# Cross-attention on a decoder layer: scores on four 32-row strips of the array, values in one run, and one written order for four engines

## The chip, the cores and the metric

The kernel runs on one core of a Trainium2 chip. The metric is device time in microseconds of one execution; three runs of the kernel before gave 1502.5, 1503.64 and 1507.64 us, a median of 1503.64. Engines are named as the profile names them: PE (TensorE; PEld are its weight loads), DVE (VectorE), ACT (ScalarE), POOL (GpSimd), SP (the sync engine, here only a DMA queue).

## The reference, cut to what matters

One decoder layer with the norm after each part, batch 2, 2048 tokens, width 512, 16 heads of 32:

```python
x = layernorm(x + ssd(x))                  # state-space mixer: Y[0] / norm @ W_out.T
x = layernorm(x + xattn(x, ctx))           # 16 heads, ctx has 77 rows, causal mask, softmax
x = layernorm(x + slots(x))                # 16 slots read x, 16 experts (512-2048-512), x reads the slots

# xattn
q = (x @ q_w + q_b);  k = (ctx @ k_w + k_b);  v = (ctx @ v_w + v_b)     # split in 16 heads of 32
att = softmax(mask(q @ k.T / sqrt(32)));  y = att @ v;  return y @ o_w + o_b
```

The change lies in the second line and the part of the third in which the slots read x (dispatch and collect below).

## The kernel before, in words

There are four stages, one behind the other. The first computes the state-space mixer and, between its steps, small set-ups (`setup()`): keys `kbh`/`kbl` and values `vt` of both batches among them. The second, here called the attention stage, is the one that the change rewrites. The third streams 192 weight slabs of 1 MB of the 16 experts through 23 slab places in SBUF. The fourth lets the tokens read the slots and writes the output.

Most matrices are held as a pair of fp32r tiles, the rounded value (`h`) and the rest (`l`). A product of two pairs is three matmuls (`three`): over a contraction of 512 that is 12 matmuls.

The attention stage goes over 16 token tiles n of 256 rows (`TB`), each as two strips s of 128 rows. One tile consists of these pieces; the letters are those that the changed source uses:

- load: DMAs of x, of the mixer's output `Ud` and of its factor `fd` (12 in all, on SP's queue)
- S, `scaled`: POOL multiplies, ACT rounds, POOL takes the rest
- O, `out_proj`: 12 matmuls of 512 columns, then DVE adds and the norm's steps on DVE and ACT
- X, `x1_transposed`: four PE transposes, ACT and DVE split them; POOL adds the output bias
- Q, `queries`: 24 matmuls of 256 columns for two groups of four heads, ACT and DVE split
- W, `weigh`: scores and softmax of four heads per call. Four heads share a matmul: `kbh` holds the keys of four heads in a block diagonal of 128 rows by 4 x 77 columns, and three matmuls of 308 columns (h by h, h by l, l by h) give the scores of four heads. Then a maximum on DVE, exponentials on ACT (for odd groups a subtraction and a sum on DVE), a reciprocal on DVE, a product on POOL
- G, `gather`: four PE transposes of the weights, copied to `pt` by ACT (three of four groups) or DVE (group 2)
- V, `values`: four matmuls per group into 32 columns of the array each; with the fourth group the result is split
- P, `o_proj`: 12 matmuls of 512 columns, norm, x2 written to HBM by a DMA that ACT issues, split
- Y, `x2_transposed`; D, `dispatch` (24 matmuls of 256 columns, running maximum and sum); T, `p_transposed`; C, `collect` (12 matmuls of 512 columns into the sums `Z`)

PSUM's eight banks are one for `y` (values), two for `mm` (O, Q, P, D, C), two for `tr` (transposes) and two for `sc` (scores).

The order in which the pieces are emitted is a table of eight beats per tile (`plan`), with written-out lists for the first and last pieces (`head`, `drain`). The whole program then goes through a scheduler with a timeline of its own, which decides the order of the instructions on each engine; that is why pieces lie interleaved on PE, for instance scores between the matmuls of a query block.

Expert slabs are placed in the order of `first`; a slab's DMA waits until the tiles of the attention stage that lie in the same SBUF bytes are done with, and SP's queue runs in order.

Of the kernel before, what the change touches and what calls it, by code (L numbers as in the profile page):

```python
# [16 lines left out]
S = 77  # L17
NE, FF = 16, 2048
# [3 lines left out]
TB = 256  # L22
# [12 lines left out]
DEFPLAN = [  # L35
    ["W", "V", ["scaled", 0, 0], ["x2_transposed", 3, 1], ["queries", 1, 0], "G"],
    ["W", "V", ["scaled", 0, 1], ["dispatch", 3], "G"],
    ["W", "V", ["o_proj", 2, 0], "G"],
    ["W", "V", ["p_transposed", 3], ["queries", 1, 1], "G"],
    ["L", "W", "V", ["x2_transposed", 2, 0], ["out_proj", 0, 0], "G"],  # L40
    ["W", "V", ["out_proj", 0, 1], "G"],
    ["W", "V", ["x1_transposed", 0, 0], ["o_proj", 2, 1], "G"],
    ["W", "V", ["x1_transposed", 0, 1], ["collect", 3], "G"]]
# [33 lines left out]
def weave(flows, depth, lag):  # L77
# [3 lines left out]
    while flows or live:  # L81
# [4 lines left out]
        for f in list(live):  # L86
# [6 lines left out]
TUNED = {'plan': [['W', ['x2_transposed', 3, 1], 'V', 'G'], ['V', 'W', 'G', ['scaled', 0, 0]],  # L93
          ['G', ['out_proj', 0, 0], ['queries', 1, 0], 'W', 'V', ['dispatch', 3]], ['W', ['o_proj', 2, 0], ['queries', 1, 1], 'G', 'V'],
          ['G', 'V', 'W', ['scaled', 0, 1], ['x2_transposed', 2, 0]], ['V', ['p_transposed', 3], 'W', 'G'],
          ['W', 'V', ['out_proj', 0, 1], ['x1_transposed', 0, 0], 'G'],
          ['V', ['x1_transposed', 0, 1], ['o_proj', 2, 1], 'L', 'G', 'W', ['collect', 3]]],
 'E': {'uf': 2,
# [15 lines left out]
 'lg': 1,  # L114
 'lv': 2,
 'dv': [1, 3],
 'first': 'ABCD067451892GH3JIFEKLM',
# [63 lines left out]
 'head': [['load', 0], ['scaled', 0, 0], ['out_proj', 0, 0], ['load', 1], ['scaled', 0, 1], ['scaled', 1, 0], ['x1_transposed', 0, 0],  # L181
          ['out_proj', 0, 1], ['out_proj', 1, 0], ['x1_transposed', 0, 1], ['queries', 0, 0], ['queries', 0, 1], ['weigh', 0, 0, 0], ['load', 2],
          ['weigh', 0, 0, 2], ['gather', 0, 0, 0], ['scaled', 1, 1], ['weigh', 0, 0, 1], ['values', 0, 0, 0], ['out_proj', 1, 1], ['gather', 0, 0, 2],
          ['x1_transposed', 1, 0], ['gather', 0, 0, 1], ['values', 0, 0, 1], ['weigh', 0, 0, 3], ['x1_transposed', 1, 1], ['weigh', 0, 1, 0],
          ['values', 0, 0, 2], ['gather', 0, 1, 0], ['weigh', 0, 1, 1], ['weigh', 0, 1, 2], ['scaled', 2, 0], ['out_proj', 2, 0], ['gather', 0, 0, 3],
          ['queries', 1, 0], ['weigh', 0, 1, 3], ['values', 0, 0, 3], ['gather', 0, 1, 1], ['o_proj', 0, 0], ['gather', 0, 1, 2], ['values', 0, 1, 0],
          ['queries', 1, 1], ['scaled', 2, 1], ['weigh', 1, 0, 0], ['gather', 0, 1, 3], ['x1_transposed', 2, 0], ['weigh', 1, 0, 1],
          ['values', 0, 1, 1], ['values', 0, 1, 2], ['values', 0, 1, 3], ['x2_transposed', 0, 0], ['gather', 1, 0, 0], ['weigh', 1, 0, 2],
          ['values', 1, 0, 0], ['out_proj', 2, 1], ['gather', 1, 0, 1], ['load', 3], ['values', 1, 0, 1], ['weigh', 1, 0, 3], ['o_proj', 0, 1],
          ['x1_transposed', 2, 1], ['gather', 1, 0, 2], ['x2_transposed', 0, 1], ['weigh', 1, 1, 0], ['values', 1, 0, 2], ['gather', 1, 0, 3],  # L190
          ['scaled', 3, 0], ['values', 1, 0, 3], ['weigh', 1, 1, 1], ['gather', 1, 1, 0], ['out_proj', 3, 0], ['weigh', 1, 1, 2], ['queries', 2, 0],
          ['gather', 1, 1, 1], ['values', 1, 1, 0], ['dispatch', 0], ['o_proj', 1, 0], ['queries', 2, 1], ['weigh', 1, 1, 3], ['gather', 1, 1, 2]],
 'drain': [['values', 12, 1, 1], ['gather', 12, 1, 3], ['values', 12, 1, 2], ['weigh', 13, 0, 0], ['scaled', 14, 1], ['x2_transposed', 12, 0],
           ['values', 12, 1, 3], ['weigh', 13, 0, 1], ['p_transposed', 11], ['gather', 13, 0, 0], ['x1_transposed', 14, 0], ['weigh', 13, 0, 2],
           ['values', 13, 0, 0], ['out_proj', 14, 1], ['gather', 13, 0, 1], ['values', 13, 0, 1], ['x1_transposed', 14, 1], ['load', 15],
           ['o_proj', 12, 1], ['gather', 13, 0, 2], ['weigh', 13, 1, 0], ['weigh', 13, 0, 3], ['weigh', 13, 1, 1], ['values', 13, 0, 2],
           ['collect', 11], ['x2_transposed', 12, 1], ['gather', 13, 0, 3], ['gather', 13, 1, 0], ['values', 13, 0, 3], ['scaled', 15, 0],
           ['out_proj', 15, 0], ['gather', 13, 1, 1], ['weigh', 13, 1, 2], ['values', 13, 1, 0], ['dispatch', 12], ['queries', 14, 0],
           ['weigh', 13, 1, 3], ['gather', 13, 1, 2], ['scaled', 15, 1], ['o_proj', 13, 0], ['queries', 14, 1], ['values', 13, 1, 1],
           ['gather', 13, 1, 3], ['values', 13, 1, 2], ['weigh', 14, 0, 0], ['x2_transposed', 13, 0], ['p_transposed', 12], ['values', 13, 1, 3],  # L200
           ['weigh', 14, 0, 1], ['gather', 14, 0, 0], ['weigh', 14, 0, 2], ['values', 14, 0, 0], ['out_proj', 15, 1], ['x1_transposed', 15, 0],
           ['gather', 14, 0, 1], ['values', 14, 0, 1], ['x1_transposed', 15, 1], ['o_proj', 13, 1], ['gather', 14, 0, 2], ['weigh', 14, 0, 3],
           ['collect', 12], ['x2_transposed', 13, 1], ['weigh', 14, 1, 0], ['gather', 14, 0, 3], ['values', 14, 0, 2], ['values', 14, 0, 3],
           ['weigh', 14, 1, 1], ['queries', 15, 0], ['gather', 14, 1, 0], ['gather', 14, 1, 1], ['weigh', 14, 1, 2], ['dispatch', 13],
           ['values', 14, 1, 0], ['weigh', 14, 1, 3], ['o_proj', 14, 0], ['queries', 15, 1], ['gather', 14, 1, 2], ['values', 14, 1, 1],
           ['gather', 14, 1, 3], ['values', 14, 1, 2], ['x2_transposed', 14, 0], ['values', 14, 1, 3], ['weigh', 15, 0, 0], ['p_transposed', 13],
           ['weigh', 15, 0, 1], ['o_proj', 14, 1], ['gather', 15, 0, 0], ['weigh', 15, 0, 2], ['values', 15, 0, 0], ['gather', 15, 0, 1],
           ['weigh', 15, 0, 3], ['gather', 15, 0, 2], ['x2_transposed', 14, 1], ['values', 15, 0, 1], ['collect', 13], ['weigh', 15, 1, 0],
           ['weigh', 15, 1, 1], ['values', 15, 0, 2], ['weigh', 15, 1, 2], ['gather', 15, 0, 3], ['values', 15, 0, 3], ['gather', 15, 1, 0],
           ['gather', 15, 1, 1], ['dispatch', 14], ['values', 15, 1, 0], ['weigh', 15, 1, 3], ['o_proj', 15, 0], ['gather', 15, 1, 2],  # L210
           ['values', 15, 1, 1], ['gather', 15, 1, 3], ['x2_transposed', 15, 0], ['values', 15, 1, 2], ['values', 15, 1, 3], ['p_transposed', 14],
           ['o_proj', 15, 1], ['collect', 14], ['x2_transposed', 15, 1], ['dispatch', 15], ['p_transposed', 15], ['collect', 15]],
 'pme': 0,
 'b1': 27,
# [3 lines left out]
 'x2': 2,  # L218
 'zt': 2,
 'qb': 2}  # L220
# [3 lines left out]
def tile_decoder(ctx, tc, a, out, dbg=None, upto=9, opt=None):  # L224
# [56 lines left out]
    kbh, kbl = ([kv_[b].tile([128, 4, 4 * S], FR, name=f"kb{t}{b}") for b in range(B)] for t in "hl")  # L281
# [11 lines left out]
    with ExitStack() as st:  # L293
# [121 lines left out]
        def setup():  # L415
# [20 lines left out]
            for b in range(B):  # L436
                for h in range(2):
                    m2 = slice(2 * h, 2 * h + 2)
                    kf = sb.tile([128, 2, 4, S], FP, tag="sw", bufs=2, name="kf")
                    pool.memset(kf, 0.0)  # L440
                    for r in range(4):
                        sr = slice(32 * r, 32 * r + 32)
                        dve.tensor_copy(kf[sr, :, r, :], kst[sr, m2, b * S:b * S + S])
                    split(kbh[b][:, m2].rearrange("p m (r s) -> p m r s", s=S), kbl[b][:, m2].rearrange("p m (r s) -> p m r s", s=S), kf, pool)
                    yield
# [254 lines left out]

    with ExitStack() as st:
        psb = {tag: st.enter_context(tc.tile_pool(name="b_" + tag, bufs=n, space=PSUM, reuse_waits="tile"))
               for tag, n in (("y", 1), ("mm", 2), ("tr", 2), ("sc", 2))}
        sbq, sb1, sb0 = (st.enter_context(tc.tile_pool(name=nm, bufs=1, side="right", reuse_waits="tile"))
                         for nm in ("b_q", "b_x1T", "b_in"))
        sbz, sbx, sb = (st.enter_context(tc.tile_pool(name=nm, bufs=1, side="right", reuse_waits="tile"))
# [125 lines left out]
        def values(n, s, hg):  # L832
            b = n // NT
            if hg == 0:
                ts[n]["y", s] = PT("y", bufs=1)
# [95 lines left out]
        def period(p):  # L931

            for q8, items in enumerate(PLAN):
                for it in items:
# [8 lines left out]
                    if 0 <= op_[1] < N:  # L943
                        yield op_
# [650 lines left out]
```

## Time and profile before

| what | value |
|---|---|
| median of 3 runs | 1503.64 us |
| the profiled execution's own time | 1507.68 us |
| its span, first to last instruction | 1505.3 us |
| mean granted PE clock | 0.949 |
| first stage, 0 to 305 us: PE, DVE busy; DMA share | 277.36, 262.41; 0.90 |
| attention stage, middle, 480 to 780 us: PE, DVE, ACT busy | 298.27, 244.62, 179.89 |
| expert stage, 928 to 1410 us: PE busy; DMA share, GB/s | 396.08; 1.00, 409 |
| last stage, 1410 to 1505 us: PE, DVE busy | 78.19, 75.88 |

How to read it: the profile is one execution, with its time beside the runs' median. Busy times of PE count pipelined matmuls, so a busy PE may still have room; the start-to-start times of its timeline tell what one instruction costs in a stream. "Waits" are idle stretches of an engine with the instruction whose end let it go on. The "chain of waits" is the work that ended last, followed back from the end. A row such as `ACT pt L234 <- PE tr L828: 20.1, 24, 2.3` reads: ACT's copy to `pt` waited 20.1 us in 24 waits for PE's transposes, 2.3 us at the longest.

### The profile page before, as it was taken

The page shows a single profiled execution, that of the slowest core. Times are in us where ns is not written, and L with a number is a line of the kernel's source. Part 1 is how long each engine was busy: PE and PEld are TensorE (multiplying, and loading weights), DVE is VectorE, ACT ScalarE, POOL GpSimd, SP SyncE. Part 2 cuts the span into 40 slices and gives each one's busy share as a digit, 9 for nine tenths or more (in the row PEclk, how much of TensorE's full clock was granted, in tenths as well). Part 3 has the DMA queues.
Part 4 walks back from the last instruction along what each step waited for, and adds up shares of the span by engine and source line. Part 5 has one row for each costly group of instructions (what it writes and reads, how often), then busy time and mean ns, then how long its engine had stood idle before and what let it go on. Part 6 is the DMA issues. An engine that isn't in the chain of part 4 may idle for free.

```text
span 1505.3 us, 27732 instructions
## 1 busy us (share of the span) xinstructions
PE 1351.7 (90%) x10442; PEld 994.8 (66%) x10442; DVE 912.4 (61%) x2150; ACT 620.1 (41%) x1685; POOL 447.5 (30%) x496
## 2 busy tenths in 40 slices
PE   7899999979999999999999997948987977889896
PEld 6788889867878888888888875205653544532365
DVE  7997997857788888888887764002111111134497
ACT  5534544525655566565656552001010000034256
POOL 4634543634444444444443311000000000000045
PEclk9999999988999999999999998969998998999899
DMA  9889978993212121322210249998999999999547
GB/s 319 210 196 239 231 198 213 242 273 92 72 57 63 58 63 57 92 57 65 64 43 15 71 153 358 363 416 363 399 418 420 418 418 419 418 421 420 226 145 261
DMA packets 188061, 339.64 MB, mean 226 GB/s; under 512 B 12347, under 2 KB 135739, under 8 KB 163096
## 3 DMA queue, kind: packets, MB, share of 16 engines
q1 hardware_dynamic: 171632, 311.25, 59.7%
q10 hardware_dynamic: 16296, 26.62, 5.2%
q8 instruction: 83, 1.36, 0.4%
q14 instruction: 50, 0.41, 0.1%
HBM read 299.56 MB, written 38.27 MB: 224 GB/s over the span
## 4 chain that ended last, share of the span: by engine, by line
PE 58%; DVE 17%; DMA 15%; ACT 5%; issue 3%; POOL 1%; SPq 1%; ACTq 0%; POOLq 0%; DVEq 0%
PE mm L231 26%; DMA ew<-in_e_W 10%; PE up L231 6%; PE pj L231 4%; PE tr L828 3%; DVE X L530 3%; PE yac L231 3%; PE sc L231 3%; PE y L231 2%; DMA ew<-in_e_Wg 2%; PE fo L231 1%; PE uu L231 1%; DVE C L530 1%; PE gp L231 1%; ACT pp L818 1%
## 5 line engine op out<-in xcount | busy, mean ns | idle before, releaser
L231 PE MATMUL up<-ew,hT 128*32 128x512 f32 x944 | 131.3, 639 | 35.5 <-DMA ew<-in_e_W 32.1
L820 POOL TENSOR_TENSOR pp<-pp,den 128x308 f32<-128x308 f32 x128 | 89.4, 703 | 158.6 <-DVE den L819 106.2
L1185 POOL MEMSET aT<- 128x512 f32 x16 | 8.3, 524 | 404.7 <-PE yac L231 403.0
L1176 ACT ACTIVATE sv<-up 128x512 f32<-128x512 f32 x32 | 19.1, 597 | 247.2 <-PE up L231 234.2
L231 PE MATMUL mm<-xTh,cqh 128*128 128x256 f32 x256 | 76.3, 308 | 26.1 <-ACT xTh L234 26.1
L231 PEld LDWEIGHTS up<-ew,hT 128*32 128x32 f32 x944 | 27.2, 113 | 101.8 <-issue 66.0
L1235 DVE TENSOR_TENSOR Qc<-mm,vec 128x512 f32<-128x512 f32 x32 | 22.1, 691 | 113.3 <-PE mm L231 113.3
L242 DVE TENSOR_TENSOR xTl<-tr,xTh 128x512 fp32r<-128x512 f32 x32 | 21.3, 689 | 109.2 <-ACT xTh L234 109.1
L828 PE MATMUL tr<-cst,pp 128*77 128x128 f32 x512 | 81.9, 285 | 1.9 <-DVE x1Tl L724 1.2
L234 ACT COPY pt<-tr 77x512 f32<-77x512 f32 x96 | 55.7, 583 | 63.2 <-PE tr L828 35.4
L231 PE MATMUL mm<-x1Th,w30h 128*128 128x256 f32 x256 | 76.7, 301 | 5.0 <-ACT x1Th L723 2.6
L818 ACT ACTIVATE pp<-sc,mx 128x77 f32<-128x77 f32 x240 | 75.5, 327 | 12.2 <-DVE mx L815 11.4
L231 PEld LDWEIGHTS mm<-xTh,cqh 128*128 128x128 f32 x256 | 51.3, 205 | 40.4 <-ACT xTh L234 29.5
L231 PE MATMUL mm<-xTl,cqh 128*128 128x256 f32 x256 | 76.6, 301 | 1.2 <-DVE xTl L242 1.2
L231 PE MATMUL mm<-x1Tl,w30h 128*128 128x256 f32 x256 | 74.4, 291 | 0.5 <-DVE x1Tl L724 0.5
L231 PE MATMUL mm<-xTh,cql 128*128 128x256 f32 x256 | 74.8, 294 | 0.0
L231 PE MATMUL mm<-x1Th,w30l 128*128 128x256 f32 x256 | 73.8, 288 | 0.0
L828 PEld LDWEIGHTS tr<-cst,pp 128*77 128x77 f32 x512 | 60.5, 150 | 16.8 <-issue 11.1
L530 DVE SCALAR_TENSOR_TENSOR X<-raw,vec,X 128x256 f32<-128x256 f32 x80 | 66.4, 876 | 5.5 <-ACT X L526 5.0
L231 PE MATMUL yac<-ew,aT 128*32 128x512 f32 x488 | 65.1, 652 | 4.7 <-issue 4.2
L746 POOL TENSOR_TENSOR ut<-ut,fb 128x512 f32<-128x512 f32 x32 | 41.2, 1291 | 73.7 <-DMA ut<-Ud 43.2
L242 POOL TENSOR_TENSOR yyl<-ut,yyh 128x512 fp32r<-128x512 f32 x32 | 41.1, 1285 | 68.3 <-ACT yyh L234 67.5
(376 smaller groups left out, 4329.2 us busy)
## 6 DMA issues: line engine op xcount, KB each, us to landing
ew<-in_e_W SPq DMA_DIRECT2D x119, 1024.0 KB, 15.0
ew<-in_e_Wg SPq DMA_DIRECT2D x60, 1024.0 KB, 12.9
BS<-scrBc SPq DMA_DIRECT2D x48, 256.0 KB, 4.9
CS<-scrC SPq DMA_DIRECT2D x48, 256.0 KB, 6.3
xs<-in_xT SPq DMA_DIRECT2D x32, 256.0 KB, 5.7
xt<-in_x SPq DMA_DIRECT2D x32, 256.0 KB, 2.7
ut<-Ud SPq DMA_DIRECT2D x32, 256.0 KB, 3.3
fb<-fd SPq DMA_DIRECT2D x128, 64.0 KB, 3.1
```

Source lines behind the costliest of these rows:

```text
L231: return pe.matmul(o, lhsT=l, rhs=r, start=start, stop=stop, **kw)
L234: (act.copy, dve.tensor_copy, pool.tensor_copy)[e](o, i)
L242: (lo_eng or dve).tensor_tensor(lo, src, hi, ALU.subtract)
L530: dve.scalar_tensor_tensor(dst, raw[:, j, 1 + t:1 + t + TB], w4[:, t:t + 1], dst, ALU.mult, ALU.add)
L746: (act, dve, pool)[EN.get('uf', 1)].tensor_tensor(ut, ut, fb, ALU.mult)
L818: act.activation(pp[:, r, :], sv[:, r, :], AF.Exp, bias=mx[:, h:h + 1], accum_out=den[:, h:h + 1])
L820: (act, dve, pool)[EN.get('d%d' % hg, 2)].tensor_tensor(pp, pp, den[:, h4].unsqueeze(2).to_broadcast([128, 4, S]), ALU.mult)
L828: pe.transpose(tp[0:S, r * 128:r * 128 + 128], pp[:, r, :], ident)
L1176: last["silu"] = act.activation(sv, up, AF.Silu)
L1185: pool.memset(aT, 0.0)
L1235: dve.tensor_tensor(Qc[b][:, mp * 2:mp * 2 + 2, t1:t1 + TB], qq, vec[:, V_CQ + mp * 2:V_CQ + mp * 2 + 2].unsqueeze(2).to_broadcast([128, 2 ...
```

## The change

- *Scores on four strips of rows.* The keys are no longer a block diagonal. `kbh`/`kbl` hold each group of heads in 80 columns (`SP`), head r in partitions 32r to 32r + 31. `weigh(n, s)` now does all 16 heads of a strip in one call with 48 matmuls of 80 columns, each over 32 contraction rows; head r of every group lands in bank r of a score tile of four banks, of which there is one.
- *Values in one run.* `values(n, s)` does the 16 matmuls of a strip together, into an `mm` bank; the `y` bank is gone, so PSUM is two `mm`, two `tr`, four `sc`.
- *Order.* Every piece is now its PE part, and generators for its steps on the other engines. `serve` walks a string of letters (`ORDER`), PE's order, with times of each step (`WORK`) and buffer counts (`ROOM`), and returns all steps sorted by the time at which its model starts them. The steps are emitted in that order, and from the thirteenth PE piece on each instruction of PE, ACT, DVE and POOL is tied to the one before it on its engine, so that the scheduler keeps the order. `plan`, `head` and `drain` are gone.
- *Moved and resized.* All `pt` copies are on ACT (32 were on DVE). load(n + 1) is issued behind the first DVE step of O(n, 0). `pt` has five buffers instead of three, the pairs of `x2` four instead of two. The set-up of `kf` is one copy per batch instead of eight. The order of the slab places (`first`) is another, and the slabs of `d_Wv`, `d_Wo` are 4 and 3 instead of K and L.

Score matmuls in the program: 1536 where there were 384.

```diff
-    kbh, kbl = ([kv_[b].tile([128, 4, 4 * S], FR, name=f"kb{t}{b}") for b in range(B)] for t in "hl")
+    kbh, kbl = ([kv_[b].tile([128, 4, SP], FR, name=f"kb{t}{b}") for b in range(B)] for t in "hl")
...
-                for h in range(2):
-                    m2 = slice(2 * h, 2 * h + 2)
-                    kf = sb.tile([128, 2, 4, S], FP, tag="sw", bufs=2, name="kf")
-                    pool.memset(kf, 0.0)
-                    for r in range(4):
-                        sr = slice(32 * r, 32 * r + 32)
-                        dve.tensor_copy(kf[sr, :, r, :], kst[sr, m2, b * S:b * S + S])
-                    split(...)
+                kf = sb.tile([128, 4, SP], FP, tag="sw", bufs=2, name="kf")
+                pool.memset(kf, 0.0)
+                dve.tensor_copy(kf[:, :, 0:S], kst[:, :, b * S:b * S + S])
+                split(kbh[b], kbl[b], kf, pool)
...
-        def weigh(n, s, hg):
...
-            sc = PT("sc")
-            for k, (l, r) in enumerate(((qh, kbh[b]), (qh, kbl[b]), (ql, kbh[b]))):
-                mm(sc[:, 0:4 * S], l[:, hg % 2, ss], r[:, hg, :], k == 0, k == 2)
+        def weigh(n, s):
...
+            sc = scp.tile([128, 4, 512], FP, tag="sc", bufs=1, name="sc")
+            for g in range(4):
+                qh, ql = ts[n]["q", g // 2]
+                for k, (l, r_) in enumerate(((qh, kbh[b]), (qh, kbl[b]), (ql, kbh[b]))):
+                    for r in range(4):
+                        sr = slice(32 * r, 32 * r + 32)
+                        mm(sc[:, r, g * SP:g * SP + SP], l[sr, g % 2, ss], r_[sr, g, :], k == 0, k == 2)
...
-        def values(n, s, hg):
...
-            for r in range(4):
-                h = hg * 4 + r
-                mm(yp[32 * r:32 * r + 32, hg * 128:hg * 128 + 128], vt[b][:, 32 * h:32 * h + 32], pt[:, r, :], True, True)
+        def values(n, s):
+            yh, yl = ts[n]["yv", s] = hi_lo("yv", [128, 4, 128], 1)
+            yp = PT("mm")
+            for h in range(H):
+                r, g = h % 4, h // 4
+                mm(yp[32 * r:32 * r + 32, g * 128:g * 128 + 128], vt[n // NT][:, 32 * h:32 * h + 32], ts[n]["pt", 4 * s + g][:, r, :],
+                   True, True)
...
+ORDER = ("OOXXQOQXWOGGGGWVOXPGGQGGQXVWOYGPGGGXWVOYQGPGDQGTGWVXYOPGGCGGWVXOCYGPGQDGGQTYVWXOPGGCGGWVXOCYPGGDQGGQ"
+             "TVYWXPOCGGCGGWVXO"
+         + 7 * "YPDGGQGGQTVYWXPOGGCGGWVXOC"
+         + "YPDGGQGGQTVYWXPOGGCGGWVOXCYPDGGQGGQTVYWPOGCGGWGXOVGCYPXDGGQGQVTXWPYOGGCGGWXVCYGQPGDGGQVTWPYGCGGGWVCY"
+             "PGGGGVDYPTCYDCTCC")
...
+        plan = serve(ORDER, N, group=NT)
+        start = [o[0] for o in plan if o[4] is None][opt.get("pin", 12)]
+        latest = {}
+        load(0)
+        for t, f, n, p, c, k in plan:
+            since = len(traced)
+            if c is None or f == "S" and k == 0:
+                chains[f, n, p] = work[f](n, p)
+            if c is not None:
+                next(chains[f, n, p][c])
+            if t >= start:
...
+                for i_ in traced[since:]:
+                    if i_.engine in latest:
+                        tc.add_manual_dep(i_, latest[i_.engine].name, mybir.DependencyInfo(
+                            mybir.DependencyClass.NoSync, mybir.DependencyReason.DATA), reason="order")
+                        latest[i_.engine] = i_
...
- 'first': 'ABCD067451892GH3JIFEKLM',
+ 'first': 'ABCD59876JKL210IEFGH43M',
```

## The prediction

> **What bounds the kernel now.** I read the page first, then the windows by stage, the waits of the attention stage, its chain of waits, and last the sync queue's timeline around the stage's end. The page's first lines and the windows (busy us of each engine, granted clock, DMA share, GB/s):
>
> ```profile
> span 1505.3 us, 27732 instructions
> PE 1351.7 (90%) x10442; PEld 994.8 (66%) x10442; DVE 912.4 (61%) x2150; ACT 620.1 (41%) x1685; POOL 447.5 (30%) x496
> ...
> 305.00:360.00 55.00, 44.46 (x300) 35.46 (x301) 37.95 (x85) 20.45 (x67) 29.40 (x27) 0.83 0.76 228
> ...
> 480.00:630.00 150.00, 149.37 (x1140) 127.06 (x1140) 121.85 (x326) 90.77 (x305) 63.78 (x65) 1.00 0.24 71
> ...
> 880.00:928.00 48.00, 42.12 (x290) 32.91 (x289) 25.35 (x70) 19.37 (x56) 9.84 (x12) 0.93 0.66 246
> 928.00:1410.00 482.00, 396.08 (x2922) 194.28 (x2920) 95.04 (x189) 71.35 (x115) 8.06 (x16) 0.91 1.00 409
> ```
>
> The attention stage (305 to 923) is TensorE's: 149.37 of 150 us busy in its middle, VectorE at 122, the DMA engines at a quarter. The expert stage behind it is the DMA engines': share 1.00. So a microsecond saved on TensorE in the attention stage counts only if the weight stream then starts earlier too. The waits of 480 to 800, TensorE's rows:
>
> ```profile
> PE mm L231 <- DVE ql L788: 1.8, 3, 0.6
> PE y L231 <- DVE pt L234: 0.3, 1, 0.3
> PE sc L231 <- ACT qh L787: 0.2, 1, 0.2
> ```
>
> TensorE waits 2.3 us in 320: the middle is paid for by its own instructions. The chain of waits (start, us, what) prices them:
>
> ```profile
> 478.52 0.79 PE y L231 x24
> 479.31 4.38 PE mm L231 x24
> ...
> 486.42 2.81 PE mm L231 x12
> 489.22 0.42 PE sc L231 x3
> 489.64 0.44 PE tr L828 x4
> ...
> 491.40 2.30 PE mm L231 x10
> 493.70 0.36 PE y L231 x8
> ...
> 503.15 1.42 PE mm L231 x12
> ...
> 799.91 4.38 PE mm L231 x24
> ```
>
> The same block of 24 at 479.31 and, nine token tiles on, at 799.91 gives a period of 320.6/9 = 35.62 us; sixteen tiles are 569.9. From TensorE's first attention matmul (timeline, 315.41) to its last before the slots (922.86) are 607.4 us, so head and drain cost 37.5.
>
> Adding up start-to-start times of TensorE's timeline over those nine periods, one period is: queries 6.03, o_proj 5.86, out_proj 5.60, scores 4.04, the four kinds of transposes 5.32, dispatch 3.13, collect 3.02, values 2.65 (sum 35.6).
>
> **The change, part by part.**
>
> *Scores.* Out: 12 matmuls 128x308 per strip of 128 rows, 4.04/2 = 2.02 us. In: 48 matmuls 128x80 over 32 contraction rows each, on four strips of the array. The trace shows none like them. Low end: the values, which already use four strips (of columns), go at (0.79 - 0.36)/16 = 0.027 us per record, 48 of them 1.3 us. High end: the transposes, each with a weight load of its own and 128 columns, 0.44/4 = 0.11 us, 48 of them 5.3 us. Below 1.3 nothing in the trace goes. I take the run of 24 value records, 0.79/24 = 0.033 us, the row it is nearest to in strip width and run length: 1.6, and 0.1 for the entry (a lone group of eight costs 0.36, against 0.215 inside a run): 1.7 us. Per period 2 x (2.02 - 1.7) = 0.64 saved.
>
> The Trainium skill (TensorE: Matmul & The Clock Gate, LDWEIGHTS) speaks against it: a weight load takes its columns over 1.2 GHz whatever the rows, which for 128 columns is 0.107 us, an estimate of 5.1 us per strip if loads stand in line, some 109 us over the kernel more than my price and a time near 1575; the same page lets loads for another row group run beside a matmul, and then my price stands. No run here shows row strips.
>
> *Values.* Out: eight groups of four matmuls scattered over the period, 2.65 us. In: two runs of sixteen, each 0.36 + 3 x 0.215 = 1.0. Saved 0.6. They now use an "mm" bank instead of one of their own.
>
> *Blocks no longer broken.* In the changed kernel's order on TensorE a period is Y P D GG Q GG Q T V Y W X P O GGG C GG W V X O C, and nearly every block of 12 or 24 stands unbroken (collect in sixes). Unbroken prices from the chain: 12 of 256 columns 1.42, 10 of 512 columns 2.30. Queries 4 x 1.42 = 5.68, dispatch 2.84, o_proj and out_proj 5.5 each, collect 2.76: 22.3 against 6.03 + 3.13 + 5.86 + 5.60 + 3.02 = 23.64, so 1.35 to gain. The step into a block after transposes (2.81 for 12, where 12 x 0.23 is 2.75, up to 0.09) is still paid about six times: 0.5 back. Saved 0.85.
>
> *Transposes.* The same 13 groups of four; no gain counted.
>
> Period: 0.64 + 0.6 + 0.85 = 2.1 saved, 33.5 us. Sixteen: 34 us.
>
> *What is moved.* 32 copies of transposed weights (pt) go from VectorE (0.68) to ScalarE (0.58): 1.2 us per period, hidden under ScalarE's idle time (90.8 of 150 busy). If that cover is gone they cost at most 1.2 x 16 = 19 us. The load of the next tile is issued behind out_proj's first add: 12 DMAs on the sync queue, 0.36 + 0.5 + 4 x 0.42 = 2.6 us of issue per half, some 3 us to land, needed by GpSimd nearly a period later; nothing else stands on that queue then. Scores have one buffer of four banks where they had two of one: the next scores wait for eight reads by VectorE and ScalarE (each 0.47, or four times 0.33 + 0.2), about 5 us, and come some 15 us later. Nothing for these.
>
> *The order written out.* The scheduler's freedom is replaced by one fixed order on four engines. TensorE waits 2.3 us in 320 now, so there is nothing to gain there in the middle, only to lose (a rival below). Head and drain, 37.5 now, are the part that a better order could shorten; TensorE's waits there (315 to 365 and 885 to 923) come to 10.4 and 5.8 us, and the half clock to the rest. Bounds: 16 us less, or 10 more (as many waits again). I take no difference.
>
> The clock belongs to this: 256-column matmuls start 0.21 us apart at 334 and 0.12 at 515, and the granted clock is 0.83 in the head. The skill's rule (same page, The HAM clock gate) is that some 3.4 us of idling halves the clock; the gaps in this head are 1.3 to 2.6 us each, shorter than the rule's, so the trace is stricter than the page.
>
> *Set-up of the keys (first stage).* Out: 16 copies kf on VectorE in four groups, 1.0 + 3.2 + 3.1 + 1.0 = 8.2 us; in: two copies. The slow ones stand beside a GpSimd op:
>
> ```profile
> 146.63 2.38 POOL L242 TENSOR_TENSOR xl<-xt,xh 128x1024 fp32r<-128x1024 f32 x1
> 178.55 3.07 DVE L443 COPY kf<-kst 32x154 f32<-32x154 f32 x4
> ```
>
> Two groups (2.47 and 2.34 us) are on the chain. Two copies at 0.3 to 2.7 save 2.8 to 7.6 of VectorE's 262 busy us in 305; the order of the stage shifts a little with them. I take 3 us, bounds +2 (worse) and -8.
>
> *The weight stream.* It must follow the stage's end E. Now, at E = 922.9, sixteen expert slabs and two d_W slabs are in; the queue goes on at E + 0.8, all 23 slabs are full at 938.5, and it starts again when the first expert frees one:
>
> ```profile
> 923.71 0.34 SPq L1052 DMA_DIRECT2D ewG<-in_e_W  x1
> ...
> 945.61 3.76 SPq L1052 DMA_DIRECT2D ew<-in_e_W  x4
> ```
>
> With the new slab order (ABCD59876JKL210I...) five slabs wait for the last collects, where four do now; 2.5 us more (1 MB at 409 GB/s), covered by the idle 938.5 to 945.6. So the whole stream and the final stage move with E; if the cover is gone, +2.5.
>
> **Sum.** -34 - 3 = -37 us. Against the profiled execution's own 1507.68 (span 1505.3 and 2.4 around it) that is 1470.7; that run is the slowest of those known and lies 4 us above the median of 1503.64, from which I get 1466.
>
> **Rivals.**
> 1. *Row strips don't overlap* (slower). Price: the transposes' 0.11 us per score matmul, (5.3 - 1.7) x 32 = 115 us, 1581. It decides from 0.06 us on: 37/32 = 1.15 us more per strip, 2.85 us for 48. For it: no such instruction in the trace, and 48 weight loads of 128 columns where there were 12. Against: values on column strips run at 0.027 to 0.033.
> 2. *The fixed order stalls.* VectorE is busy 122 of 150, so it has a fifth to spare, and one late add of 0.69 us holds a bank of two. Two such waits per period: 1.4 x 16 = 22 us, 1488. For it: every engine now takes its work in one order; against: TensorE hardly waits now, and VectorE loses work.
> 3. *Head and drain get shorter too*: 16 us less, 1450. For it: 16 us of waits there; against: pipeline fill is made of dependent steps.
> 4. *Nothing arrives*: the DMA-bound stage begins later relative to E, or the order loses what the matmuls gain; 1500 to 1508.
>
> **How the numbers follow.** Forecast 0.48 (own range 1456 to 1478), rival 3 0.14 (1446 to 1456), rival 2 0.18 (1478 to 1499), rival 4 0.05, rival 1 0.15. The first three make the range, 1446 to 1499, with 0.8. What a measurement can tell from no change is 0.3%, 4.5 us: faster (below 1499) is those three, 0.80; the same is rival 4, 0.05; slower is rival 1, 0.15.
>
> **What would show it.** In the profile after: a period of 33.5 us between equal query blocks; scores of 48 in 1.6 to 1.8 us; values of sixteen near 1.0; unbroken blocks of 12 at 1.42 and 2.75 to 2.81; TensorE's waits in the middle below 0.5 us per period; first attention matmul near 312, last collect near 886; the weight stream again at share 1.00 and as long as before. Wrong: scores above 2.85 us per strip, TensorE busy clearly under 99% in the middle, or a DMA gap of over 10 us after E.

## The result, and the profile after

The changed kernel takes 1575.65 us (median of four, 1572.37 to 1577.31), the kernel before beside it 1505.64: a ratio of 1.0458, interval 1.042 to 1.0496. It is 70 us slower, where 37 us less were forecast and the range ended at 1499.

The page's first lines, then the windows by stage (busy us of each engine with its instructions, granted clock, DMA share, GB/s):

```profile
span 1574.4 us, 29882 instructions
PE 1367.9 (87%) x11594; PEld 1009.9 (64%) x11594; DVE 898.1 (57%) x2104; ACT 638.7 (41%) x1715; POOL 442.3 (28%) x492
```

```profile
305.00:360.00 55.00, 44.29 (x324) 35.66 (x324) 31.28 (x68) 16.91 (x46) 20.44 (x18) 0.75 0.73 220
480.00:630.00 150.00, 133.94 (x1262) 112.82 (x1260) 106.23 (x277) 84.69 (x276) 56.47 (x59) 0.99 0.18 52
950.00:1000.00 50.00, 41.29 (x338) 33.54 (x337) 28.22 (x80) 22.73 (x68) 10.93 (x15) 0.97 0.66 243
1000.00:1482.00 482.00, 398.03 (x2946) 194.13 (x2948) 95.93 (x191) 72.05 (x116) 8.14 (x16) 0.91 1.00 412
```

Before, TensorE was busy 149.37 of these 150 us in the middle; now it is 133.94, and VectorE, ScalarE and GpSimd fell with it. No engine is the bound any more: all four wait for one another. The expert stage is as it was.

The new scores and values themselves cost what was forecast, or less. Out of TensorE's timeline (start, duration, shape, count):

```profile
579.76 0.95 PE L309 MATMUL mm<-pt,vt 77*32 77x128 f32 x28
580.64 0.66 PE L796 MATMUL tr<-cst,x 128*128 128x128 f32 x4
581.23 0.31 PE L309 MATMUL sc<-kbh,qh 32*128 32x80 f32 x4
...
582.47 0.29 PE L309 MATMUL sc<-kbh,ql 32*128 32x80 f32 x4
582.69 0.66 PE L796 MATMUL tr<-cst,x 128*128 128x128 f32 x4
```

The 48 score matmuls run from 581.23 to 582.69, 1.46 us where 1.7 was forecast; twelve groups of four start 0.11 us apart, so the four strips do overlap. The prediction weighed a serial reading of the Trainium skill's rule for weight loads (TensorE: Matmul & The Clock Gate, LDWEIGHTS), an estimate of 5.1 us; the trace does not show it.

What is new is in the waits of 480 to 780 us (engine, line, operation, releaser: us in total, times, longest):

```profile
ACT pp L934 <- DVE pp L924: 15.0, 14, 1.2
PE tr L948 <- ACT pt L951: 12.0, 10, 1.5
DVE mx L930 <- ACT pp L934: 10.2, 7, 1.5
DVE mx L922 <- ACT pp L934: 8.4, 6, 1.4
ACT pp L934 <- DVE mx L922: 8.3, 4, 2.3
PE tr L948 <- POOL pp L938: 5.9, 11, 0.7
PE mm L309 <- DVE yvl L968: 3.5, 4, 1.0
```

L930 and L922 are the maxima of even and odd chunks, L934 the exponentials of even chunks, L924 the subtractions of odd ones. A maximum needs the scores and nothing else, and yet it waits for ScalarE's exponentials of another chunk; these wait for a subtraction of another chunk. None of this is data. One strip's softmax on VectorE and ScalarE (idle time before, and its releaser, in brackets):

```profile
582.82 0.48 DVE L930 TENSOR_REDUCE mx<-sc 128x4 f32<-128x308 f32 x1
583.21 0.47 DVE L922 TENSOR_REDUCE mx<-sc 128x4 f32<-128x308 f32 x1
583.60 0.47 DVE L930 TENSOR_REDUCE mx<-sc 128x4 f32<-128x308 f32 x1
585.47 0.48 DVE L922 TENSOR_REDUCE mx<-sc 128x4 f32<-128x308 f32 x1 [1.40 <-ACT pp L934]
```

```profile
585.22 0.21 ACT L934 ACTIVATION_READ_ACCUMULATOR pp<-sc,mx 128x1 f32 x1
586.37 0.33 ACT L934 ACTIVATE pp<-sc,mx 128x77 f32<-128x77 f32 x1 [0.93 <-DVE pp L924]
```

Three maxima go through, the fourth stands until ScalarE's first exponentials (584.10 to 585.43) are over, and ScalarE's second ones then stand until VectorE's subtraction is. All eight steps (four maxima, two sets of exponentials, two subtractions) read the one score tile, and the two engines take turns at it. With one order on each engine, whatever comes behind (TensorE's copies and adds) is late too.

### The profile page after: what moved, and what is told of

Read it like the earlier page. It is cut to its first block, busy times and chain, and to the rows that moved or that the text cites. A ratio compares the mean times of both kernels' runs of the same rounds, so it can differ in the third digit from the quotient of the medians.

```text
span 1574.4 us, 29882 instructions
## 1 busy us (share of the span) xinstructions
PE 1367.9 (87%) x11594; PEld 1009.9 (64%) x11594; DVE 898.1 (57%) x2104; ACT 638.7 (41%) x1715; POOL 442.3 (28%) x492
## 4 chain that ended last, share of the span: by engine, by line
PE 40%; DVE 25%; DMA 17%; ACT 10%; issue 5%; POOL 1%; ACTq 1%; SPq 0%; POOLq 0%; DVEq 0%
PE mm L309 14%; DMA ew<-in_e_W 8%; PE up L309 6%; PE pj L309 5%; DMA ew<-in_e_Wg 4%; ACT pp L934 3%; PE yac L309 3%; DVE X L604 2%; DVE bst L810 2%; PE uu L309 1%; PE tr L948 1%; PE fo L309 1%; ACT pt L951 1%; ACT x L985 1%; DMA xr<-x2d 1%
## 5 line engine op out<-in xcount | busy, mean ns | idle before, releaser
L948 PE MATMUL tr<-cst,pp 128*77 128x128 f32 x512 | 77.7, 287 | 44.6 <-POOL pp L938 22.5
L1276 ACT ACTIVATE sv<-up 128x512 f32<-128x512 f32 x32 | 19.1, 598 | 218.9 <-PE up L309 204.7
L934 ACT ACTIVATE pp<-sc,mx 128x77 f32<-128x77 f32 x240 | 74.7, 324 | 67.8 <-DVE pp L924 32.2
L951 ACT COPY pt<-tr 77x512 f32<-77x512 f32 x128 | 69.3, 583 | 32.4 <-PE tr L948 24.5
L991 POOL TENSOR_TENSOR x2l<-x,x2h 128x512 fp32r<-128x512 f32 x32 | 41.1, 1283 | 114.0 <-ACT x2h L989 114.0
L879 POOL TENSOR_TENSOR x<-x,ob 128x512 f32<-128x512 f32 x32 | 41.1, 1287 | 110.0 <-PE tr L796 110.0
L312 ACT CAST xTh<-tr 128x512 fp32r<-128x512 f32 x32 | 18.3, 587 | 117.4 <-PE tr L1298 104.1
```

Source lines behind the costliest of these rows:

```text
L879: pool.tensor_tensor(x1, x1, ob, ALU.add)
L934: act.activation(pp[:, r, :], sv[:, r, :], AF.Exp, bias=mx[:, h:h + 1], accum_out=den[:, h:h + 1])
L948: pe.transpose(tp[0:S, r * 128:r * 128 + 128], pp[:, r, :], ident)
L951: act.copy(pt, tp[0:S, :].rearrange("p (r t) -> p r t", t=128))
L991: pool.tensor_tensor(x2l, x2, x2h, ALU.subtract)
L1276: last["silu"] = act.activation(sv, up, AF.Silu)
```

## The experiments

The first question was whether this taking of turns is the loss (theory A), or an order written with hand-overs that are too short (theory B).

**e1_bank: chunks cut by bank.** Chunk r is now the four heads whose scores lie in bank r, and each bank is a tile of its own.

```diff
-            sc = scp.tile([128, 4, 512], FP, tag="sc", bufs=1, name="sc")
+            sc = [scp.tile([128, 512], FP, tag=f"sc{r}", bufs=1, name="sc") for r in range(4)]
...
-                sv, pp = sc[:, :, hg * SP:hg * SP + S], pps[hg]
+                sv, pp = sc[hg][:, 0:4 * SP].rearrange("p (g s) -> p g s", s=SP)[:, :, 0:S], pps[hg]
...
```

> The changed kernel, but the four softmax chunks of a strip are cut by bank: chunk r is the four heads whose scores lie in bank r, where the changed kernel's chunk g took one head from each of the four banks. The score tile is four tiles of one bank. Same matmuls, same counts, same written order on all four engines. Theory A (in the changed kernel VectorE and ScalarE may not read the score banks at the same time, so their softmax reads wait for one another, and the written order passes that wait on to everything behind): the waits of ScalarE's exponentials for VectorE's subtractions and of VectorE's maxima for ScalarE's exponentials disappear, the period falls from 41.1 us to 34 to 37 us, and 16 periods give back 65 to 110 us: 1465 to 1510 us, ratio to before 0.97 to 1.005. Theory B (the order's model takes the hand-overs too short, so the order is late whatever the banks): the cross waits were only where the lateness showed; the period stays above 40 us and the time stays at 1560 to 1580 us, ratio 1.035 to 1.05.

Measured: 1520.69 us, ratio 1.0084 (1.0052 to 1.0117). VectorE's four maxima now follow one another, with ScalarE's first exponentials from 567.98 on, beside the fourth of them (timeline of e1):

```profile
566.90 0.48 DVE L930 TENSOR_REDUCE mx<-sc 128x4 f32<-128x308 f32 x1
567.29 0.47 DVE L922 TENSOR_REDUCE mx<-sc 128x4 f32<-128x308 f32 x1
567.68 0.47 DVE L930 TENSOR_REDUCE mx<-sc 128x4 f32<-128x308 f32 x1
568.07 0.47 DVE L922 TENSOR_REDUCE mx<-sc 128x4 f32<-128x308 f32 x1
```

From the first attention matmul to the last collect the stage takes 619.8 us (322.6 to 942.4) instead of 674.9. So 55 us were the turns, as theory A has it, but the run is 11 us above the end of what A expected: the period falls from 40.8 us only to 36.9 in most tiles, 37.2 on average, about the upper end of A's 34 to 37. No row of e1's waits has a maximum wait for ScalarE. What is left, in e1's window of 480 to 630 and its waits of 480 to 780:

```profile
480.00:630.00 150.00, 141.39 (x1399) 121.62 (x1398) 116.63 (x307) 89.66 (x297) 63.03 (x65) 1.00 0.20 59
```

```profile
ACT brs L814 <- DVE bmv L811: 54.3, 25, 4.1
PE tr L948 <- ACT pt L951: 12.8, 14, 1.5
PE mm L309 <- ACT pd L1022: 3.6, 8, 1.2
```

Twice per tile, behind a query block and behind a collect, TensorE's next transposes wait about a microsecond for a copy on ScalarE. ScalarE is busy 89.66 of 150: it stands in line for a norm (54.3 us of waits for `bmv`), and the copies stand behind it.

**e2_loose and e3_bank_loose: the order not tied** (`'pin': 415` instead of 12: of the 416 PE pieces only the last is tied), with the changed kernel's chunks and with chunks by bank.

> The changed kernel with its score layout, but the written order is not tied on the four engines: the scheduler's own order stands, started from the same listing. Theory A: the waits between ScalarE's and VectorE's reads of the four score banks remain, but an engine that would stand in one may take other work first; part of the loss comes back: period 36 to 39 us, 1500 to 1545 us. Theory B: tying the order is the whole loss, so the time falls to what strips were forecast to give, about 1466 to 1500 us, and cutting the chunks by bank besides (the third run) adds nothing.

> Both edits together: chunks cut by bank, and the order not tied on the engines. Theory A: without the cross waits the written order no longer hurts, so this is within 1.5% of the first run (1465 to 1520 us). Theory B: this equals the second run and is at least 3% faster than the first.

Measured: e2 1571.56 us, ratio 1.0403 (1.0354 to 1.0453); e3 1535.86, 1.0193 (1.0137 to 1.0249). Untying the order gives almost nothing back with the shared tile (less than A allowed, and far from B), and costs 15 us without it, which puts e3 above the 1520 that A allowed. Tying the engines was not the fault.

**e4_costs: the model's durations set to measured ones**, on e1, with TensorE's order kept. In e1's trace a norm takes far longer than the model has it. The third buffer for `zt` (a norm's input) that the expectation below names is not in this edit; the durations are all that changes. The change, shortened:

```diff
-NORM = [("D", .69, .77), ("A", .28, .39), ("D", .57, .67)]
+NORM = [("D", .8, .92), ("A", .43, .56), ("D", 1.25, 1.35)]
...
```

> The first run (chunks by bank) with the same order on TensorE, but the event model's durations set to what the first run's trace shows: a normalisation takes 0.92 + 0.56 + 1.35 us on VectorE, ScalarE, VectorE where the model had 0.77 + 0.39 + 0.67; ScalarE stands 1.22 us in the step that writes x2 and issues its transfer (model 0.71); VectorE 1.3 us in the maxima of dispatch (model 1.12). This moves instructions on VectorE, ScalarE and GpSimd; the rotation of zt gets a third buffer, since more normalisations now overlap in the listing. Theory A2 (what is left of the loss is ScalarE standing in line for a normalisation that the model has too short, with the copies of transposed weights behind it): TensorE's two gaps of about 1 us per tile behind collect and behind queries shrink, period 35.5 to 36.5 against 37.5, time 1490 to 1510 us. Theory B2 (the order on TensorE itself leaves too little between transposes and their copies, whatever the others do): the gaps move, period 37 to 38, time 1512 to 1530 us.

Measured: 1516.23 us, ratio 1.0079 (1.0052 to 1.0106): no difference from e1. The gaps only move: TensorE waits 14.1 us in eight waits for VectorE's x1 (`tr L796 <- DVE x L869`), where it waited 12.8 for ScalarE. Theory A2 falls, and B2's expectation came true: the order on TensorE itself has to change.

**e5_reordered: TensorE's order written anew for the measured durations**, by the kernel's own event model. Its beginning and end are new too; here are the repeated part and the two buffer counts that change with it (`zt`, and `pp`, the softmax's weights):

```diff
-         + 7 * "YPDGGQGGQTVYWXPOGGCGGWVXOC"
+         + 7 * "GPYQQGDGXWGYOTGVWGGCGPVOXC"
...
- 'zt': 2,
+ 'zt': 3, 'pp': 8,
```

> As the run above (chunks by bank, measured durations), and the order on TensorE is written anew for these durations: the single pieces of work are the same, no transposes stand three in a row, and queries, values and collect come later after what feeds them; eight softmax buffers in place of five. The model puts the end of the stage 40 us earlier than with the old order (566 against 606 in its own terms). Theories A and A2 together (bank wait, and an order made with durations that are too short, make the whole loss against the forecast): period 34 to 35 us, TensorE busy 98% and more in the middle, 1465 to 1490 us, ratio to before 0.97 to 0.99. Rival (strips and unbroken runs save nothing on TensorE, and before is at the floor): 1500 us or more.

Measured: 1481.89 us, ratio 0.9843 (0.9822 to 0.9863), inside the expected range and faster than the kernel before. The stage takes 572.9 us (319.7 to 892.6), the period is 34.5, and TensorE is nearly full again (e5's window, as above):

```profile
480.00:630.00 150.00, 146.97 (x1485) 127.47 (x1482) 129.55 (x331) 97.02 (x323) 67.21 (x70) 1.00 0.21 63
```

The two buffer counts were not tried without the order, so what is said of the order below is said of all three together.

**e6_reordered_4bank: the changed kernel's chunks under the new order.**

> The run above with the chunks cut as in the changed kernel: each chunk has one head from each of the four banks, in one tile of four banks. Nothing else differs. Theory A (VectorE's and ScalarE's reads of the same banks are made to take turns): 30 to 60 us slower than the run above, with ScalarE's exponentials again waiting for VectorE's subtractions and the reverse. Rival (the wait hurts only in the order that the changed kernel has): within 10 us of the run above.

Measured: 1544.15 us, ratio 1.0256 (1.0228 to 1.0284), 62 us above e5, just over the 30 to 60 expected. The turns cost about the same under a good order, and their rows are back in e6's waits (480 to 780):

```profile
DVE mx L930 <- ACT pp L934: 12.2, 8, 2.2
ACT pp L934 <- DVE mx L922: 11.2, 12, 1.5
```

**e9_one_tile: chunks by bank, but in one tile of four banks.** This asks whether it is the banks or the tile. On e5:

```diff
-            sc = [scp.tile([128, 512], FP, tag=f"sc{r}", bufs=1, name="sc") for r in range(4)]
+            sc_ = scp.tile([128, 4, 512], FP, tag="sc", bufs=1, name="sc")
+            sc = [sc_[:, r, :] for r in range(4)]
```

> The reordered run (e5_reordered) with one score tile of four banks in place of four tiles of one bank; the chunks are still cut by bank, so no bank is ever read by two engines at a time. If it is the banks that VectorE and ScalarE may not share, this equals the reordered run, 1477 to 1487 us. If it is the tile (the program makes the two engines' reads of one score tile take turns, whatever banks they touch), it equals e6_reordered_4bank, 1535 to 1550 us, with ScalarE's exponentials waiting for VectorE's maxima and subtractions of other chunks and VectorE for ScalarE.

Measured: 1547.2 us, ratio 1.028 (1.0245 to 1.0315), as e6. The waits of 480 to 780 are those of the shared tile, although no chunk touches another's bank (line numbers are one higher in this kernel); e5 has no row in which a maximum waits for ScalarE:

```profile
DVE mx L931 <- ACT pp L935: 11.5, 8, 1.7
ACT pp L935 <- DVE mx L923: 11.4, 14, 1.5
```

So what makes the engines take turns is a wait that the program carries for each score tile. The Trainium skill states why such a wait is needed at all (PSUM — Partial Sum Buffer, PSUM bank collisions raise a hardware error): two engines may not be at the same bank and quadrant at once, reads against reads included. This rule spoke against the change, and the prediction did not weigh it. The runs agree with it in e1, where chunks in different banks do not wait, and go further in e9: here the wait goes by tile, wider than the page's bank. No run here lets both engines read one bank at once, so what the chip would do then is not shown.

**e8_no_strips: the strips undone, all else as in e5.** Keys lie in blocks again, 12 matmuls of 308 columns per strip, each chunk's scores in a tile of its own:

```diff
...
-                    for r in range(4):
-                        sr = slice(32 * r, 32 * r + 32)
-                        mm(sc[r][:, g * SP:g * SP + SP], l[sr, g % 2, ss], r_[sr, g, :], k == 0, k == 2)
+                    mm(sc[g][:, 0:4 * S], l[:, g % 2, ss], r_[:, g, :], k == 0, k == 2)
...
```

> The reordered run (e5_reordered) with the strips undone: the keys are laid out in blocks again as in the kernel before (128 rows, 308 columns, set up by four copies per half), a strip of 128 tokens takes 12 score matmuls of 128x308 in place of 48 of 128x80, and each chunk's scores still lie in a bank and tile of their own. Order, durations in the model, values in one run and buffers stay. Theory A (strips and values are worth on TensorE what the traces show: 4.0 us of scores per tile before, 2.9 to 3.0 on strips): 1.0 us per tile comes back where TensorE is the bound, 12 to 18 us in all, and the set-up of the keys 0 to 5: 1494 to 1505 us. Rival (the order written for these durations makes the whole gain over before, strips none): within 5 us of the reordered run, 1477 to 1487 us.

Measured: 1474.19 us, ratio 0.9803 (0.9769 to 0.9837): below both expectations. The two were then run together on one chip, as e10 (strips) and e11 (none).

> The reordered run (e5_reordered) once more, beside the next one on the same chip. By the traces of e5_reordered and e8_no_strips, strips save 0.62 us of scores per tile and give 0.35 back where TensorE goes from transposes into them, so a period is 34.5 against 34.7 us and strips should lead by 3 to 4 us over sixteen tiles, if the start of the stage and the weight stream behind it take the same. If what the earlier runs showed holds (first attention matmul 4 us later, since the set-up of the keys lets the scheduler issue the last projection weights beside the stage's first loads; the weight stream 10 us longer in the one profile), strips lose 5 to 10 us. Expected: 1478 to 1484 us.

> The run without strips (e8_no_strips) once more, on the same chip as the run above. If strips gain what the middle of the stage shows and the rest was the execution, this is 3 to 4 us slower than the run above; if the start of the stage and the weight stream decide, it is 5 to 10 us faster: 1472 to 1477 us.

Measured: e10 1485.62 us, 0.9864 (0.9836 to 0.9891); e11 1476.23, 0.9804 (0.9772 to 0.9835). e10 lies 1.6 us above its expected range, e11 inside its own. Without strips it is 9.4 us faster, and this is the best version: 30 us below the kernel before beside it (1506.24). TensorE's timelines of e10 and e11 show what strips do there:

```profile
516.91 0.31 PE L309 MATMUL sc<-kbh,qh 32*128 32x80 f32 x4
...
518.16 0.29 PE L309 MATMUL sc<-kbh,ql 32*128 32x80 f32 x4
518.38 1.10 PE L948 MATMUL tr<-cst,pp 128*77 128x128 f32 x8
```

```profile
541.39 0.41 PE L309 MATMUL sc<-kbh,qh 128*128 128x308 f32 x1
...
543.04 0.30 PE L309 MATMUL sc<-kbh,ql 128*128 128x308 f32 x1
543.17 0.93 PE L950 MATMUL tr<-cst,pp 128*77 128x128 f32 x7
```

48 on strips take 1.47 us, 12 without 1.78. But before, where the 12 lay in four groups between other work, they took 2.02: 0.24 of what a strip of tokens saves comes from the run, 0.31 from the strips. And the step from transposes into strips is 0.20 us (in e10 the last transpose starts at 543.58, the first score at 543.78), into full-width scores 0.03; from values it is 0.20 in both. The Trainium skill names a price here (TensorEngine Tiling (Array Packing), Tiling Modes): changing the tiling mode drains the engine; these 0.2 us agree with it. The period ends up at 34.5 with strips and 34.8 without; the whole stage at 572.9 and 575.9 us (e5, e10) against 579.4 and 580.4 (e8, e11).

The 4.5 to 6.5 us that strips save in the stage are lost at both ends of it. At its start the first matmul comes 16.7 us behind the first load with strips (e5; 16.6 in e10), 12.3 and 13.0 without, 12.3 before. SP's queue, first before and then e10:

```profile
305.38 2.65 SPq L740 DMA_DIRECT2D fb<-fd  x4
```

```profile
303.20 0.43 SPq L723 DMA_DIRECT2D wr<-in_W_outT  x1
...
309.49 5.38 SPq L838 DMA_DIRECT2D fb<-fd  x4
```

With the smaller set-up of the keys the scheduler puts a load of projection weights 3.7 us ahead of the stage's first loads, and the four transfers that GpSimd waits for take 5.38 us to issue instead of 2.65. That the one makes the other was not tried. In this pair another 7.1 us lie ahead of the first load itself (306.9 in e10, 299.8 in e11); between e5 and e8 there is no such difference (303.0 in both), so it is not put down to the strips. And the weight stream has a slow stretch, 100 to 180 us behind the last collect (windows of e10, then e11):

```profile
999.40:1079.40 80.00, 76.80 (x593) 46.37 (x589) 17.03 (x30) 8.44 (x15) 1.58 (x3) 0.98 0.96 373
```

```profile
993.20:1073.20 80.00, 70.52 (x548) 40.26 (x549) 14.96 (x28) 8.06 (x14) 1.05 (x2) 0.96 1.02 418
```

There the queue waits for slabs that TensorE has not freed: 29.7 us for `up` in e10, 19.1 in e11. Strips alone do not make this: from the last collect to the end, the changed kernel and e1 to e4, all with strips, take 576.2 to 582.8 us, the new order with strips (e5, e6, e9, e10) 584.8 to 587.4, and without (e8, e11) 576.5 and 579.5. That the 23 slab places fill in another order would fit; why it comes out so was not settled.

## Why the prediction was wrong

Against its own span of 1468.3 us (1505.3 - 37), the profiled execution is 106.1 longer, in four pieces: first load 3.4 later than forecast (303.6 against 300.15), from there to the first matmul 3.9 more, first matmul to last collect 674.9 against 573.1, and the rest 3.0 shorter. The 101.8 of the stage are the error.

- **Scores' buffer** (*What is moved*: "the next scores wait for eight reads by VectorE and ScalarE ... Nothing for these"): this step failed. It asked who waits for the tile to come free, and not what two engines do to each other while they both read it. That measures 674.9 - 619.8 = 55.1 us (e1), and 62 in e6 against e5.
- **The order written out** ("nothing to gain there in the middle, only to lose ... I take no difference") and **rival 2**, its price: the right rival, but counted as two waits of 0.69 us on TensorE's banks, 22 us. From e1's 619.8 to e5's 572.9, 46.9 us were the order's (with its two buffers), and the places were other ones: transposes behind queries and collect, waiting for copies that stood behind norms. Both steps were read off a trace in which TensorE hardly waited, which says nothing of what a new order does.
- **Scores, values, blocks, transposes** (2.1 us per tile): scores and values cost what was forecast or less (1.46 for 1.7 and 1.0 for 1.0), but in e5, with the two faults gone, only 1.1 of the 2.1 came. Adding up start-to-start times over five tiles of e5 (530 to 739 us, without the tile at the change of batch), as the prediction did, gives a period of 34.5 where 33.5 was forecast: scores 2.9 for 3.4, values 2.0 for 2.0, blocks 23.3 for 22.8, transposes 6.3 for 5.3. So the blocks gave back 0.4 and not 0.85, and the transposes, for which nothing was counted, cost 1.0 more, a third of it the two steps into strips (without strips, e8, they take 5.95).
- **Head and drain** ("I take no difference"): 572.9 less 16 x 34.5 leaves 20.9 us for them in e5, where 37.5 were taken over from before. This is rival 3's 16 us. That e5's stage of 572.9 us meets the forecast's 607.1 - 34 = 573.1 is therefore luck: two errors of some 16 us cancel.
- **What carries the gain**: put down to the strips in part (0.64 per tile). e5 against e8 and e10 against e11 show 0.3 per tile in the period for them. Of the 27.7 us by which e8's stage is shorter than before (579.4 against 607.1), about half is the period (34.8 for 35.6), with scores and values in one run and blocks unbroken, and half head and drain under the new order. These parts were not tried one by one.
- **Set-up of the keys** (-3): not seen. The two copies that are left take 0.31 us each, where sixteen took some 8 in all, but the first load comes at 303.6 after 303.2, and the first matmul 4.3 later than before. With the same set-up the first load lies anywhere from 300.7 (e4) to 306.9 (e10), so single executions can't show 3 us.
- **The weight stream** (+0 to 2.5): mis-sized in both directions. From the last collect to the end it took 579.8 us in the changed kernel, 582.8 before, 586.2 in e5, 576.5 in e8.
- **Rival 1** (1581) came close to the measured time, by a mechanism that is not there: strips overlap.

## What to carry to other kernels

When a change gives one tile to readers on two engines, list the pairs of readers, not only who waits for the buffer: if they may not read at once, cut the work so that each reads a tile and a bank of its own. An order written out for several engines deserves durations from a trace of that very kernel, serial chains of one-column operations and an engine's own DMA issues included; then make the order itself anew, for here the durations alone changed nothing (e4), and with the order made anew from them the stage became 46.9 us shorter (e5). And before an instruction is replaced by a narrower one, run the old one unbroken under the same order: here that was the faster of the two, by 9.4 us.

## What the runs showed of the hardware

- Four 32-row strips of the array with loads of their own: groups of four 32x80 matmuls start 0.11 us apart, 0.028 each; into strips from full-width transposes 0.20 us, out of them to the next start 0.21.
- One-column operations on VectorE are long and uneven: the first of the four that end a norm has a mean of 0.52 us and takes 0.22 to 0.90 in one tile of e1. Whether GpSimd's work beside it does that was not tried.
- ScalarE is held for 1.22 us by an activation of 0.82 and the DMA that it issues itself behind it: in e1 x2 starts at 593.91, its transfer is issued from 594.76 to 595.09, and the next copy starts at 595.13, with transposes on TensorE waiting for it.
